# Idle 256-column products on TensorE where the schedule lets it rest, in a transformer, router and scan block

## The chip, the cores and the metric

The kernel runs on one core of a Trainium2 chip. The metric is the device time of one execution in microseconds (us), the lowest being best. Three executions of the kernel before gave 2063.22, 2063.66 and 2065.26 us, so their median is 2063.66 us. The profile is of a further execution.

## The reference, cut to what matters

Sixteen sequences of 512 tokens and 256 features pass through four stages, each with a residual addition on a freshly normalised input:

```python
x = x + attention(layernorm(x))     # 16 heads of 16, causal softmax, rms norm inside
x = x + ffn(layernorm(x))           # base + shared low rank + 6 routed low-rank experts, best 2 of 6
x = x + ssm(layernorm(x))           # conv of 4, gates, a scan over 512 steps with state 16 x 256
x = x + ffn(layernorm(x))           # the same weights again
```

All data is float32. The sequences are independent of each other; within one, every stage needs the one before it.

## The kernel before, in words

The whole program is unrolled. For each sequence the functions `attention`, `routed`, `scan` and `routed` again record *operations*: a `Plan.op` has an engine, an estimated cost, a function that issues its instructions, and the tiles that it reads and writes. Nothing is issued while they are recorded. Then `Plan.order()` plays all operations of all sequences through a small model of the core: each engine does one operation at a time, an operation is ready when those it depends on are done, places in SBUF and PSUM are counted, and of the ready ones an engine takes the one with the lowest *turn* (`STARTS` of its sequence plus a number from `TURNS`). The operations in the order of their starts in that model are the program: the loop under `tc.manual_schedule()` calls their functions one by one, and each engine's queue runs in that order. The model's times decide the order and nothing else[...].

Four setup functions run in that last loop, each ahead of the first operation of its stage. `for_attention` (ahead of the first operation of stage 2) loads and scales weights and issues a small transpose (L359) and two products `wo` by `sg` (L474) on TensorE. They are not in the model.

TensorE (PE) writes two kinds of places in PSUM: `one`, four buffers of one bank each (128x512 float32), and `sc`, a single place of four banks. The operations that matter below:

- `turned`: four transposes of a normalised sequence (`xhA`, `xhR`) by `ident` into a `one` (L505), which ScalarE (ACT) copies to `xtA`, `xtR` or `xpad` (L508).
- `four`: scores of four heads into `sc`, L566, and masks, L568. In the first use VectorE (DVE) reduces the scores to `negm` (L637). In the second, ACT takes the exponent into `pt` (L585). The next `four` needs `sc` again, so these alternate with it.
- `turn` of `negm` (L645), then `qm` on DVE (L650); `weigh`, the weighted values (L590); `back` (L601).
- In `scan`: GpSimd (POOL) multiplies at L856 and L867 on `dd`, which arrives by DMA from `drows`; ACT's exponent L861; DVE's scan L864; and `add`, eight PE instructions at L874 for two `dd`, after which the `dd` are free for the next transfers.
- `products` (L474) are all plain matrix products; a float32 product is recorded as two matmul instructions.

The PE estimate in the model is `pe(n, k) = k * 2 * (n / 1200 + 0.02)` us, a transpose group is 0.66, and `act(512)` is 0.63. The first PE operation of the plan is sequence 0's `turned`. Ahead of it the model knows: the load of `x`, 0.7 us of issue, 2.3 of transfer and 2.0 of latency; four times 0.6 us of statistics; 1.65 us of POOL; four times 0.593 us of ACT.

Of the kernel before, what the change touches and what calls it, by code (L numbers as in the profile page):

```python
# [10 lines left out]
F32 = mybir.dt.float32  # L11
# [6 lines left out]
P = 128  # L18
# [31 lines left out]
class Buf:  # L50


    def __init__(self, plan, res, make):
        self.plan, self.res, self.make = plan, res, make
        self.tile, self.users, self.taken = None, 0, False
        self.done = {}
# [11 lines left out]
class Plan:  # L68
# [6 lines left out]

    def __init__(self, places):
        self.places, self.ops, self.seq, self.stage = dict(places), [], 0, 0

# [45 lines left out]
    def order(self):  # L126

        first = {}
        for o in self.ops:
            o.turn = STARTS[o.seq] + (TURNS or [0] * len(self.ops))[o.num - first.setdefault(o.seq, o.num)]  # L130
        free, busy, table, link, port = dict(self.places), {}, None, 0.0, False
        kept = {}
        ready = {}
        for o in self.ops:
            ready.setdefault(o.eng, [])
            busy.setdefault(o.eng, False)
            if not o.left:
                bisect.insort(ready[o.eng], (o.turn, o.num, o))
        events, out = [], []
        now, tick = 0.0, 0  # L140
        while True:
            for eng, heap in ready.items():
                if busy[eng] or not heap:
                    continue
                until, what = kept.get(eng, (None, None))

                picked, turns = None, heap
                if eng == "ACT":
                    turns = sorted(heap, key=lambda i: (i[0] + CHANGE * (i[2].table not in (None, table)), i[1]))
                for item in turns:  # L150
                    if until is not None and not self.wanted(item[2], what):
                        cost = item[2].cost + 1.3 * (item[2].table not in (None, table))
                        if now + cost > until + OVER:
                            continue
                    need = {}
                    for b in item[2].bufs:
                        if not b.taken:
                            need[b.res] = need.get(b.res, 0) + 1
                    if not (item[2].port and port) and all(free[k] >= v for k, v in need.items()):
                        picked = item[2]  # L160
                        heap.remove(item)
                        break
                if picked is None:
                    continue
                o = picked
                for b in o.bufs:
                    if not b.taken:
                        b.taken = True
                        free[b.res] -= 1
                cost = o.cost  # L170
                if o.table is not None:
                    cost += 1.3 * (o.table != table)
                    table = o.table
                if until is not None and self.wanted(o, what):
                    del kept[eng]
                if isinstance(o.then, Op):
                    kept[o.then.eng] = (now + cost + o.lat, o.then)
                elif o.then is not None:
                    kept[o.then[0]] = (now + cost + o.lat, o.then[1])
                busy[eng] = True  # L180
                port = port or o.port
                out.append(o)
                end = now + cost
                done = end + o.lat
                if o.load:
                    link = max(link, end) + o.load
                    done = link + o.lat
                tick += 2
                heapq.heappush(events, (end, tick, "free", o))
                heapq.heappush(events, (done, tick + 1, "done", o))  # L190

            late = [eng for eng, (at, what) in kept.items() if at + 0.3 < now and not busy[eng]]
            for eng in late:
                del kept[eng]
            if late:
                continue
            if not events:
                if not kept:
                    break
                kept.clear()  # L200
                continue
            now = events[0][0]
            while events and events[0][0] <= now:
                _, _, kind, o = heapq.heappop(events)
                if kind == "free":
                    busy[o.eng] = False
                    if o.port:
                        port = False
                    continue
                for b in o.bufs:  # L210
                    b.users -= 1
                    if not b.users:
                        free[b.res] += 1
                for x in o.after:
                    x.left -= 1
                    if not x.left:
                        bisect.insort(ready[x.eng], (x.turn, x.num, x))
        assert len(out) == len(self.ops), "operations wait for each other's places"
        self.span = now
        return out  # L220


@with_exitstack
def tile_block(ctx: ExitStack, tc: tile.TileContext, a: dict, out: bass.AP):
# [4 lines left out]
    nc = tc.nc  # L229
# [16 lines left out]
    ps = ctx.enter_context(tc.tile_pool(name="ps", bufs=1, space=PSUM))  # L246
# [5 lines left out]
    def tile_of(name, shape, dtype=F32):  # L252
        return const.tile(shape, dtype, name=name)
# [7 lines left out]
    ident, identb = tile_of("ident", [P, P]), tile_of("identb", [P, P], BF)  # L261
# [166 lines left out]
    banks = {"one": (4, [P, 512]), "sc": (1, [P, G, 512])}  # L428
# [3 lines left out]
    plan = Plan(places)  # L432
# [463 lines left out]
    with tc.manual_schedule():  # L896
        done = 0
        for o in plan.order():

            while done < o.stage:  # L900
                setups[done]()
                done += 1
            o.fn()


# [44 lines left out]
```

## Time and profile before

| | |
|---|---|
| median of the runs | 2063.66 us |
| profiled execution, its own time | 2066.51 us |
| its span, first to last instruction | 2064.7 us |
| mean granted TensorE clock | 0.954 |
| PE busy | 1801.9 us, 87% |
| DVE / POOL / ACT busy | 1513.4 / 1371.1 / 1194.0 us |

The profiled execution is 2.85 us above the median of the three, and 1.8 us of its own time lie outside its span. "PEclk" in a table of stretches is the TensorE clock that was granted, as a share of full speed, meaned over the stretch. In a list of instructions, a row has its start, its time, engine, line, what it wrote and read, and in brackets how long the engine had been idle before it and which instruction ended that. Rows of the same line that follow closely are merged, and "x8" is their number; ends of matmuls are modelled.

### The profile page before, as it was taken

The numbers are of one execution on the slowest core, as the hardware profiler recorded it, in microseconds if no ns is written. First come the engines' busy times: TensorE is split into PE (matmuls) and PEld (weight loads), VectorE is DVE, ScalarE is ACT, GpSimd is POOL, SyncE is SP. The second block draws the span as 40 slices with busy tenths as digits, with TensorE's granted clock in tenths as the row PEclk, the third lists the DMA queues.
The fourth block names the chain that finished last, engine by engine and source line by source line (L and its number), as shares of the span: only waits on it lengthen the run. The fifth ranks groups of instructions, "written<-read, shape, count | busy, mean of one in ns | idle before, by whom it ended". The sixth has DMA issues, their size and how long they took to land. (4 is left out here: it accounts for less than half of the span.)

```text
span 2064.7 us, 34733 instructions
## 1 busy us (share of the span) xinstructions
PE 1801.9 (87%) x13253; PEld 953.8 (46%) x13253; DVE 1513.4 (73%) x2479; ACT 1194.0 (58%) x1685; POOL 1371.1 (66%) x814
## 2 busy tenths in 40 slices
PE   4788789999999999999999999999999999996455
PEld 2244344555455454545455454545554454544123
DVE  4335677878788787878788787878788787876563
ACT  2236556565666757565666667575666766564431
POOL 3001784949587685859597785859596785848693
PEclk8789899999999999999999999999999999998766
DMA  3000956848494866847494867849493957747791
GB/s 93 1 1 22 216 122 155 197 127 210 109 233 109 216 164 167 205 137 191 110 231 100 225 153 175 204 120 212 110 231 95 228 143 186 183 125 183 186 222 31
DMA packets 113064, 316.35 MB, mean 153 GB/s; under 512 B 17809, under 2 KB 36610, under 8 KB 112898
## 3 DMA queue, kind: packets, MB, share of 16 engines
q1 hardware_dynamic: 112194, 313.99, 62.5%
q8 instruction: 105, 1.72, 0.4%
q14 instruction: 61, 0.50, 0.1%
q10 hardware_dynamic: 704, 0.14, 0.0%
HBM read 287.87 MB, written 26.21 MB: 152 GB/s over the span
## 5 line engine op out<-in xcount | busy, mean ns | idle before, releaser
L864 DVE TENSOR_TENSOR_SCAN dd<-one,dd 128x512 f32<-128x512 f32 x512 | 607.9, 1212 | 185.2 <-ACT one L861 88.3
L856 POOL TENSOR_TENSOR dd<-dd,bc 128x1024 f32<-128x1024 f32 x256 | 603.6, 2361 | 194.0 <-DMA dd<-drows 156.8
L867 POOL TENSOR_TENSOR dd<-dd,bc 128x1024 f32<-128x1024 f32 x256 | 601.9, 2358 | 86.2 <-DVE dd L864 80.4
L637 DVE TENSOR_REDUCE negm<-sc 128x4 f32<-128x512 f32 (+3 forms) x256 | 380.4, 1486 | 154.0 <-PE sc L568 153.7
L861 ACT ACTIVATE one<-dd,am 128x512 f32<-128x512 f32 x512 | 344.3, 689 | 249.4 <-DVE dd L864 108.9
L585 ACT ACTIVATE pt<-sc 128x2048 f32<-128x2048 f32 (+3 forms) x256 | 316.3, 1235 | 189.0 <-PE sc L568 187.8
L487 POOL TENSOR_SCALAR rs<-mv 128x4 f32<-128x4 f32 x64 | 12.3, 193 | 364.2 <-DVE mv L482 361.4
L566 PE MATMUL sc<-qm,kT 32*128 32x512 f32 (+3 forms) x2048 | 214.1, 488 | 37.8 <-ACT pt L585 28.4
L566 PE MATMUL sc<-kT,qT 32*128 32x128 f32 (+3 forms) x2048 | 217.0, 494 | 30.5 <-DVE negm L637 25.9
L568 PEld LDWEIGHTS <-identb 128*128 128x128 bf16 x2048 | 117.4, 98 | 232.4 <-issue 217.2
L874 PE MATMUL one<-dd,ysel 128*32 128x512 f32 x1024 | 172.7, 633 | 55.5 <-POOL dd L867 46.4
L590 PE MATMUL one<-pt,vv 128*32 128x512 f32 (+3 forms) x2048 | 191.6, 449 | 8.1 <-DVE dd L864 7.9
L566 PEld LDWEIGHTS sc<-qm,kT 32*128 32x128 f32 x2048 | 80.9, 185 | 181.5 <-ACT pt L585 120.4
L474 PE MATMUL one<-base,xtR 128*128 128x256 f32 x512 | 139.5, 395 | 18.6 <-DVE dd L864 18.0
L566 PEld LDWEIGHTS sc<-kT,qT 32*128 32x128 f32 x2048 | 82.0, 187 | 156.8 <-DVE negm L637 63.3
L494 ACT ACTIVATE xhR<-x,nm,rs 128x256 f32<-128x256 f32 x192 | 99.4, 588 | 53.2 <-POOL nm L490 53.1
L528 DVE TENSOR_TENSOR x<-one,x 128x512 f32<-128x512 f32 x128 | 86.4, 675 | 34.7 <-PE one L474 34.5
L474 PEld LDWEIGHTS one<-base,xtR 128*128 128x128 f32 x512 | 94.5, 194 | 36.8 <-DVE dd L864 21.5
L481 DVE BATCH_NORM_STATS2 st<-x 128x6 f32<-128x256 f32 x256 | 103.7, 405 | 4.8 <-DMA x<-in_x_dram 4.1
L568 PE MATMUL sc<-mask_q,identb 128*128 128x128 bf16 x1024 | 103.7, 225 | 0.0
L568 PE MATMUL sc<-mask_k,identb 128*128 128x128 bf16 x1024 | 102.8, 224 | 0.0
L505 PE MATMUL one<-ident,xhR 128*128 128x128 f32 x384 | 61.9, 290 | 35.2 <-ACT xhR L494 27.7
(132 smaller groups left out, 2449.4 us busy)
## 6 DMA issues: line engine op xcount, KB each, us to landing
dd<-drows SPq DMA_DIRECT2D x512, 512.0 KB
x<-in_x_dram SPq DMA_DIRECT2D x16, 512.0 KB
drows<-dt SPq DMA_DIRECT2D x32, 256.0 KB
drows<-sg SPq DMA_DIRECT2D x32, 256.0 KB
bc<-brows SPq DMA_DIRECT2D x16, 512.0 KB
out_dram<-x SPq DMA_DIRECT2D x16, 512.0 KB
brows<-few SPq DMA_DIRECT2D x16, 64.0 KB
wo<-in_Wo_dram SPq DMA_DIRECT2D x2, 256.0 KB
```

Source lines behind the costliest of these rows:

```text
L474: nc.tensor.matmul(o[:, lo:hi], lhsT=lhsT, rhs=rhs, start=n == 0, stop=n == len(todo) - 1)
L481: nc.vector.bn_stats(st()[:, t, :], x()[:, t, :])
L566: nc.tensor.matmul(sc()[:, g, 0:n], lhsT=lhsT(g), rhs=rhs(g), start=True, stop=False)
L568: nc.tensor.matmul(sc()[:, g, at : at + P], lhsT=identb, rhs=mask, start=False, stop=True)
L585: o.then = op("ACT", act(G * n), lambda pt=pt, sc=sc, n=n: nc.scalar.activation(pt(), sc()[:, :, 0:n], AF.Exp), r=[sc], w=[pt], table="exp")
L590: nc.tensor.matmul(av()[rows(g), kt * P : T], lhsT=vals()[:, kt, G * j + g, :], rhs=pt()[:, g, :], start=kt == 0, stop=kt == NT - 1,)
L637: o.then = op("DVE", dve(G * n), lambda t=t, n=n, sc=sc, nm=nm, s=s: nc.vector.tensor_reduce(nm()[:, t, :, 1 - s, 0:1], sc()[:, :, 0:n], A ...
L856: op("POOL", pool(1024), lambda dd=dd: nc.gpsimd.tensor_tensor(dd()[:, :, 1, :], dd()[:, :, 1, :], both(0), ALU.mult), port=True, r=[(bc, ...
L861: op("ACT", act(512) + 0.07, lambda i=i, k=k, dd=dd, dec=dec: nc.scalar.activation(dec(), dd()[:, i, 0, :], AF.Exp, scale=am[:, k + 4 * i ...
L864: op("DVE", 1.22, lambda i=i, dd=dd, dec=dec: nc.vector.tensor_tensor_scan(dd()[:, i, 1, :], dec(), dd()[:, i, 1, :], 0.0, ALU.mult, ALU.a ...
L867: op("POOL", pool(1024), lambda dd=dd: nc.gpsimd.tensor_tensor(dd()[:, :, 1, :], dd()[:, :, 1, :], both(1), ALU.mult), port=True, r=[(bc, ...
L874: nc.tensor.matmul(sums()[rows(g), :], lhsT=ysel[:, m, :], rhs=four[g]()[:, g % 2, 1, :], start=m == 0, stop=m == 3)
```

## The change

`order()` also notes when PE begins and ends each operation in the model (`runs`), and how many `one` places are free at each time (`room`). After the plan is made, `resting` walks through PE's rests in the model. At a point of a rest it looks back 3.4 us. If the model's PE was busy for less than 72% of that, idle products put there included, if the rest has 0.55 us left, and if a `one` place is free throughout those 0.55 us, it books one idle product of 0.45 us; otherwise it moves on by 0.1 us. The count is kept with the PE operation that ends the rest. The issuing loop puts that many products ahead of it, each into a fresh `one` tile: `ident` as weights, `ident` twice (256 columns) as the moving operand. Nothing reads the result. The order of the other operations is unchanged, and no idle product is issued before the first setup. Since the loop over setups stands ahead of the new lines, products booked ahead of the first PE operation stand behind `for_attention`'s own PE work in PE's queue.

```diff
+    SPAN, BUSY, IDLE, EDGE = 3.4, 0.72, 0.45, 0.1
...
+        runs, room = [], [(0.0, free["one"])]
...
+                if eng == "PE":
+                    runs.append((now, end, o))
...
         self.span = now
+        self.rests = self.resting(runs, room)
         return out
+
+    def resting(self, runs, room):
+
+        rests, last, at, k = {}, [], 0.0, 0
+        for begin, end, o in runs:
+            while at + self.IDLE + self.EDGE <= begin:
+                while k + 1 < len(room) and room[k + 1][0] <= at:
+                    k += 1
+                i, free = k + 1, room[k][1]
+                while i < len(room) and room[i][0] < at + self.IDLE + self.EDGE:
+                    free = min(free, room[i][1])
+                    i += 1
+                last = [x for x in last if x[1] > at - self.SPAN]
+                worked = sum(b - max(a, at - self.SPAN) for a, b in last)
+                if free > 0 and worked < self.BUSY * self.SPAN:
+                    rests[o.num] = rests.get(o.num, 0) + 1
+                    last.append((at, at + self.IDLE))
+                    at += self.IDLE
+                else:
+                    at += self.EDGE
+            last.append((begin, end))
+            at = max(at, end)
+        return rests
...
             while done < o.stage:
                 setups[done]()
                 done += 1
+            for _ in range(plan.rests.get(o.num, 0) if done else 0):
+                one = ps.tile([P, 512], F32, tag="one", name="one", bufs=banks["one"][0])
+                nc.tensor.matmul(one[:, 0 : 2 * P], lhsT=ident, rhs=ident.unsqueeze(1).to_broadcast([P, 2, P]), start=True, stop=True)
             o.fn()
```

More of the change, by code (lines that the diff above doesn't have):

```diff
@@ L169, in order @@
                         free[b.res] -= 1
+                        if b.res == "one":
+                            room.append((now, free["one"]))
                 cost = o.cost
@@ L213, in order @@
                         free[b.res] += 1
+                        if b.res == "one":
+                            room.append((now, free["one"]))
                 for x in o.after:
```

## The prediction

> **What bounds the kernel now.** I read the page's slices first, then the same by stretches for PE alone, to see where TensorE has work and at what clock.
>
> ```profile
> core 0: us, PE busy (x), PEclk, DMA share, GB/s
> 0.00:22.33 22.33, 3.64 (x13) 1.00 0.70 195
> 22.33:118.00 95.67, 69.59 (x438) 0.71 0.03 5
> 118.00:300.00 182.00, 152.39 (x1189) 0.94 0.41 97
> 300.00:1850.00 1550.00, 1456.72 (x11085) 1.00 0.69 168
> 1850.00:2028.00 178.00, 98.72 (x472) 0.74 0.80 189
> 2028.00:2064.70 36.70, 20.86 (x76) 0.73 0.04 15
> ```
>
> From 300 to 1850 us PE is busy 94% at full clock: PE bounds, and nothing about the clock can be won. The clock is lost at both ends. Next the stretches of 3.41 us around the first loss:
>
> ```profile
> 39.40:42.81 3.41, 1.47 (x12) 1.00 0.02 5
> 42.81:46.22 3.41, 1.35 (x12) 0.50 0.00 0
> ...
> 59.88:63.29 3.41, 2.96 (x13) 0.50 0.00 0
> 63.29:66.70 3.41, 3.41 (x8) 0.50 0.00 0
> 66.70:70.12 3.42, 2.86 (x30) 1.00 0.00 0
> ```
>
> The clock is either 1.00 or 0.50 and changes on a grid of 3.41 us. A stretch busy 43% (1.47 us) is followed by half speed; at half speed one busy 87% (2.96) is still followed by half speed, a full one by full speed. I laid this grid over the trace: at full clock every stretch under 50% was followed by a fall, none over 55%; at half clock nothing under 86% was followed by a rise. So keeping warm needs little more than half, warming up needs nearly all. By the grid the half clock holds 42.8 to 66.7, 76.9 to 80.4, 94.0 to 117.9; 20 us in three pieces from 213 to 292; from 1882 on, most of the time.
>
> What it costs is seen in the list of DVE, whose reductions follow `four`:
>
> ```profile
> 42.29 2.29 DVE L637 TENSOR_REDUCE negm<-sc 128x4 f32<-128x2048 f32 x1 [1.56 <-PE sc L568]
> 46.02 0.69 DVE L637 TENSOR_REDUCE negm<-sc 128x4 f32<-128x512 f32 x1 [1.44 <-PE sc L568]
> 48.58 1.23 DVE L637 TENSOR_REDUCE negm<-sc 128x4 f32<-128x1024 f32 x1 [1.87 <-PE sc L568]
> 52.10 1.76 DVE L637 TENSOR_REDUCE negm<-sc 128x4 f32<-128x1536 f32 x1 [2.29 <-PE sc L568]
> 56.58 2.29 DVE L637 TENSOR_REDUCE negm<-sc 128x4 f32<-128x2048 f32 x1 [2.72 <-PE sc L568]
> ```
>
> DVE and PE alternate: each waits for the other (one place `sc`), so PE's time is all on the path. The same shape makes DVE wait 1.56 us warm and 2.72 cold. At the end, the chain of waits runs from 1957 to 2028 through POOL and the `dd` transfers, and after 2028 mostly through PE.
>
> [...]
>
> **The change part by part.**
>
> *One product's cost.* It is two matmul instructions of 128x256 float32. Two such (`up` by `hT`) start at 293.92 and the next at 294.35: 0.43 us warm. Cold, four (`base`) start at 2052.83 and the next at 2054.54: 0.86 for two. The booked 0.45 fits the warm one. Nothing reads the result, so no other engine gets work. SP, POOL and DMA queues are passed by nothing; no transfer is added.
>
> *How many.* I applied the rule to the rests of PE in the trace, which stand in for the model's: some 175 products, about 19 before the first PE operation, 30 more up to 300 us, none from 300 to 1800, 120 after. Since the first stage runs cold in the trace and warm in the model, it gets more: I take 190. The dense middle then costs nothing, because PE never rested 28% of 3.4 us there; the cover is the rest itself. If the model's rests lie elsewhere, 15 products of 0.43 on the path are 6.5 us: bounds 0 to +6.5, taken 0.
>
> *The first batch, a loss.* In the model PE rests until the first `turned`, at 0.7+2.3+2.0+2.4+0.12+1.65+0.12+2.37+0.05 = 11.7 us. By the rule this gives six products, a pause of 1 us, six, pause, six, pause, one: 19. On the chip they stand behind the setup's PE work, which waits for weights:
>
> ```profile
> 18.93 2.08 PE L474 MATMUL one<-wo,sg 128*128 128x256 f32 x4 [0.64 <-DMA cw<-in_conv_w_dram]
> 20.80 1.80 PE L505 MATMUL one<-ident,xhA 128*128 128x128 f32 x8
> ...
> 32.37 0.50 PE L566 MATMUL sc<-kT,qT 32*128 32x128 f32 x8
> ```
>
> The transposes were ready (the last `xhA` ended at 10.85) and started as PE became free, so here 19 products are wholly on the path: two cold, 17 warm after the grid point at 22.3, 1.7+7.3 = 9.0 us. Part comes back, as PE is warm from then on. Transposes from 29.8, the first group 0.6; ACT copies 0.59, does four `xhA` (2.07) and copies 0.58: 33.7; three 512-column products of 4x0.43 (one stretch cold before): 38.9 instead of 32.4. **Loss 6.5 us**, bounds 4 and 9.
>
> *The first two heads' groups, a gain.* Cold waits of DVE before the four reductions: 1.44+1.87+2.29+2.72 = 8.3. Warm: 1.56 for the longest, 1.14 for 1024 columns (the reduction at 87.92); I estimate 1.35 and 0.9 for the others in proportion: 5.0. Gain 3.4. Waiting for L645 0.65 to 0.5. The next `four` starts at 60.33 and ACT's `pt` at 62.99, 2.66 instead of about 1.56: 1.1. Then `wq` cold delays the next `four` to 66.41, 3.4 after `pt` began, where `pt` itself needs 1.9: 1.5. Together 6.1; the stretch from 94 to 118 has the same rows: 12.2. At 76.9 to 80.4 a `four` 0.55 and a `weigh` 0.85. **Gain 13.6 us**, bounds 9 and 14. Products don't eat it: a rest of 2.4 us (DVE's 2.29) takes three, 1.3 us, and leaves 1.1, so windows stay above 60%. Had the clock fallen, three are 2.6 us and fill the rest, and the next window warms. What is late next is DVE itself, which this count already includes.
>
> *118 to 300.* 20 us cold with the same `four` rows at 214 to 223 (two of 512, 2.3 us) and shorter ones; PE isn't dense. I take **2 us gain**, bounds 0 and 4. The lead then carries through the dense middle, as order and waits there are the same.
>
> *The tail before 2028.* POOL is busy 85% of 1850:2028 and the DMA share is 0.80, so PE is off the path; only ACT's waits for cold PE in sequence 15's preparation touch it. **1 us**, bounds 0 and 3; a product batch delaying `add` could release `dd` later, about +1.
>
> *The tail after 2028.* Cold against warm rows: `add` 0.95, `wo` by `gate` 1.05, transposes 0.85, `low` 1.3, `hsc` 0.5, the last `base`/`up` 1.95: 6.6 us if all were warm. The rests before them are
>
> ```profile
> 2040.97 2.03 PE L505 MATMUL one<-ident,xhR 128*128 128x128 f32 x8 [5.57 <-ACT xhR L494]
> ...
> 2051.87 1.17 PE L754 MATMUL one<-ident,hsc 128*113 128x128 f32 x4 [5.06 <-DVE hsc L745]
> ```
>
> About eight products each, but they all run at the start of the rest, since they wait for nothing, and some 2 us stay idle at its end. A grid window falls if 1.7 us of it are idle: for 2.1 us of rest that is 2.1/3.41, six in ten. So I take 45% of 6.6: **3 us**, bounds 0 and 6.5.
>
> Sum: +6.5 −13.6 −2 −1 −3 = **−13.1 us**. The profiled execution's span goes from 2064.7 to 2051.6; its own time, 2066.51, stands 2.85 above the median, and 2063.66−13.1 gives 2050.5.
>
> **Rivals.** (a) *The first batch without the return*, slower. Products of `ident` may not count as activity, or the rests fall otherwise: then the 6.5 to 9 us ahead of the first transpose stay, nothing comes back, 2070 to 2073. For it: the batch is certain, and the path is bare there. Against: cold runs of plain products ended the half clock at 66.7 and 117.9. It decides once less than half of the 13.6 is regained. (b) *Held warm everywhere*, the tail too, and a first batch that costs 4: +4−13.6−4−3−6.5 = −23, 2040.5. Against it is the idle end of each rest. (c) *Gain at the start only, and the dense middle pays*: +6.5−13.6+6.5 = −0.6, 2063: products ahead of `four`, which needs no `one`, wait for a `one` that the model thought free. For it: the model isn't the chip; against: no rest of the trace's middle meets the rule. (d) The diff doing nothing is excluded, as the first rest alone books products.
>
> **How the numbers follow.** The forecast 0.60 (2043 to 2058); (b) 0.15; (c) 0.11; (a) and products in front of other work 0.14. 0.2%, 4.1 us, is about what a measurement of this kernel can tell from no change. Faster by more: forecast, (b) and a little of (c), 0.77; within 0.10; slower 0.13. The range takes in (b), its bounds, and (c): 2037 to 2066.
>
> **What would show it.** Right: PE clock near 1.00 from 22 to 118; the first L505 near 29.8 and the first L566 near 39, but L637 of the second head's group with waits of 1.56 for 2048 columns; the middle's PE rows unchanged; the tail's clock between 0.75 and 0.9, mean above 0.98. Wrong: the first L505 near 21 (batch not on the path), a half clock between 43 and 67, new products with waits for ACT or DVE between 300 and 1850, or POOL waiting longer for `dd` after 1940.

## The result and the profile after

The change made the kernel slower: 2083.17 us (median of 4) against 2063.44, a ratio of 1.0093 with a 95% interval of 1.0076 to 1.0110. The profiled execution took 2082.81 us, its span is 2081.0, and its mean TensorE clock rose from 0.954 to 0.983. Ratios are given beside the medians; where the two differ slightly, the ratio decides.

The stretches of PE in the kernel after (length, busy time and instructions, granted clock, DMA share, GB/s):

```profile
22.33:118.00 95.67, 81.16 (x599) 1.00 0.03 5
118.00:300.00 182.00, 160.21 (x1248) 0.97 0.42 102
300.00:1850.00 1550.00, 1458.45 (x11095) 1.00 0.69 169
1850.00:2028.00 178.00, 131.76 (x584) 0.87 0.72 170
2028.00:2064.70 36.70, 27.20 (x121) 0.81 0.09 22
```

The start is warm throughout, as wanted, and the dense middle has the same PE work as before, 1458 us against 1457. The clock of the tail is better as well (0.87 and 0.81, from 0.74 and 0.73), yet the tail is where the time went. The DMA share of 1850:2028 fell from 0.80 to 0.72, which alone says little: the early-only kernel below, which is faster than before, has 0.73 there, as its stages stand at other times.

To find the place I matched the 13253 matmuls of before with the same ones of after, idle products left out, and took the difference of their starts: +6.8 us at the first `four`, −7.1 at 124 us, −9.6 at 300, −10.1 at 1860, and then +25 at an `add` near 2021 of before's trace, +19 at 2035. So the change wins 10 us at the start, carries them through 1550 us without losing any, and loses nearly 30 in the last 200: 35 up to that `add`, of which the end gives some back.

The start, as PE's list shows it:

```profile
20.76 9.44 PE L941 MATMUL one<-ident 128*128 128x256 f32 x38
30.04 1.04 PE L541 MATMUL one<-ident,xhA 128*128 128x128 f32 x8
...
39.13 0.50 PE L602 MATMUL sc<-kT,qT 32*128 32x128 f32 x8
```

19 products (two instructions each) stand ahead of the first transpose and take 9.3 us of the bare path. What follows runs at a clock of 1.00 up to 118 us. These are DVE's reductions of the second head group, whose waits had been 1.44, 1.87, 2.29 and 2.72 us:

```profile
52.27 0.69 DVE L673 TENSOR_REDUCE negm<-sc 128x4 f32<-128x512 f32 x1 [0.92 <-PE sc L604]
54.10 1.23 DVE L673 TENSOR_REDUCE negm<-sc 128x4 f32<-128x1024 f32 x1 [1.14 <-PE sc L604]
56.67 1.76 DVE L673 TENSOR_REDUCE negm<-sc 128x4 f32<-128x1536 f32 x1 [1.35 <-PE sc L604]
59.99 2.29 DVE L673 TENSOR_REDUCE negm<-sc 128x4 f32<-128x2048 f32 x1 [1.56 <-PE sc L604]
```

The waits between 1860 and 2050 us in the kernel after (who waited for whom, us in total, times, longest):

```profile
ACT one L897 <- PE one L941: 48.3, 7, 10.0
PE one L941 <- DVE dd L900: 44.0, 13, 6.8
```

Neither line could stand there before, as L941 is new. Idle products wait for scans, and ACT's exponents wait for idle products. The list of all engines shows how, between 2012 and 2025 us:

```profile
2011.53 4.64 DVE L900 TENSOR_TENSOR_SCAN dd<-one,dd 128x512 f32<-128x512 f32 x4 [6.73 <-POOL dd L892]
2012.79 0.69 ACT L897 ACTIVATE one<-dd,am 128x512 f32<-128x512 f32 x1 [0.97 <-DVE dd L900]
...
2014.01 10.18 PE L941 MATMUL one<-ident 128*128 128x256 f32 x32 [3.56 <-DVE dd L900]
...
2023.37 2.73 ACT L897 ACTIVATE one<-dd,am 128x512 f32<-128x512 f32 x4 [9.89 <-PE one L941]
2024.12 1.06 PE L910 MATMUL one<-dd,ysel 128*32 128x512 f32 x8
2024.14 4.57 DVE L900 TENSOR_TENSOR_SCAN dd<-one,dd 128x512 f32<-128x512 f32 x4 [7.98 <-ACT one L897]
```

A place of `one` holds the exponent (L897) until the scan (L900) has read it. Sixteen products stand ahead of the `add`. The batch can begin when PE has a rest, but its products need places that scans still hold, so PE idles 3.56 us first, runs the batch until 2024.2, and only then the `add`. The next exponents come after the batch in the program and need the places that it passes through: ACT sits idle 9.89 us, then DVE 7.98 us. Half of the chain of waits from 2006 to 2050 is L941, and 36.8% are `dd` transfers. The chain shows how the two hang together, as the late `add` is followed by the issue and the transfer of the next `dd`:

```profile
2015.26 8.93 PE one L941 x30
2024.19 1.05 PE one L910 x8
...
2025.28 0.51 SPq L885
...
2025.83 6.69 DMA dd<-drows
```

POOL's waits for `dd` transfers between 1940 and 2050 us rose from 3.4 us before to 14.2, one of the signs of being wrong that the prediction had named.

### The profile page after: what moved, and what is told of

Its sections match the earlier page's. It is cut to its first block, busy times and chain, and to the rows that moved or that the text cites. A ratio compares the mean times of both kernels' runs of the same rounds, so it can differ in the third digit from the quotient of the medians.

```text
span 2081.0 us, 35605 instructions
## 1 busy us (share of the span) xinstructions
PE 1872.6 (90%) x13689; PEld 1024.0 (49%) x13689; DVE 1511.7 (73%) x2479; ACT 1194.3 (57%) x1685; POOL 1372.0 (66%) x814
## 5 line engine op out<-in xcount | busy, mean ns | idle before, releaser
L900 DVE TENSOR_TENSOR_SCAN dd<-one,dd 128x512 f32<-128x512 f32 x512 | 607.9, 1212 | 199.5 <-ACT one L897 104.2
L897 ACT ACTIVATE one<-dd,am 128x512 f32<-128x512 f32 x512 | 343.9, 689 | 272.8 <-DVE dd L900 99.6
L602 PE MATMUL sc<-kT,qT 32*128 32x128 f32 (+3 forms) x2048 | 210.8, 481 | 19.3 <-DVE negm L673 14.5
L941 PE MATMUL one<-ident 128*128 128x256 f32 x436 | 128.0, 441 | 47.3 <-DVE dd L900 44.3
L910 PE MATMUL one<-dd,ysel 128*32 128x512 f32 x1024 | 156.2, 604 | 12.7 <-issue 7.7
L941 PEld LDWEIGHTS one<-ident 128*128 128x128 f32 x436 | 90.6, 220 | 81.5 <-issue 36.5
```

The source lines that it names most:

```text
L602: nc.tensor.matmul(sc()[:, g, 0:n], lhsT=lhsT(g), rhs=rhs(g), start=True, stop=False)
L897: op("ACT", act(512) + 0.07, lambda i=i, k=k, dd=dd, dec=dec: nc.scalar.activation(dec(), dd()[:, i, 0, :], AF.Exp, scale=am[:, k + 4 * i ...
L900: op("DVE", 1.22, lambda i=i, dd=dd, dec=dec: nc.vector.tensor_tensor_scan(dd()[:, i, 1, :], dec(), dd()[:, i, 1, :], 0.0, ALU.mult, ALU.a ...
L910: nc.tensor.matmul(sums()[rows(g), :], lhsT=ysel[:, m, :], rhs=four[g]()[:, g % 2, 1, :], start=m == 0, stop=m == 3)
L941: nc.tensor.matmul(one[:, 0 : 2 * P], lhsT=ident, rhs=ident.unsqueeze(1).to_broadcast([P, 2, P]), start=True, stop=True)
```

## The experiments

Each was timed beside the kernel before. In text, "+24.7 us" is the ratio minus one, times the median of before beside it.

**Only the early, only the late products.** The rule gets a bound on the model's time: 63 products are booked early, 155 late.

```diff
-                if free > 0 and worked < self.BUSY * self.SPAN:
+                if free > 0 and worked < self.BUSY * self.SPAN and at < 1000.0:    # late: at >= 1000.0
```

> Only the 63 idle products that the model books before its 1000 us; the 155 later ones are left out. Theory A (the loss lies in the tail: a product waits for a place of `one` that a scan still holds, and a batch of up to 20 then runs ahead of an `add` that was ready): the lead of the start stays, some 10 us, so 2053 us (2051 to 2056), and the tail looks as before. Rival B (the products slow the kernel wherever they stand, or the lead is worth nothing once the transfers bound the end): 2060 to 2075.

Measured: 2056.08 us against 2061.16, ratio 0.9974 (0.9965 to 0.9984), −5.4 us: a gain, at the upper edge of what theory A forecast.

> Only the 155 idle products after the model's 1000 us. Theory A: the loss of the tail alone, without the lead of the start: 2063.4 plus 28 to 30, so 2092 us (2087 to 2096). Rival C (the tail is only late because the start shifted how the last sequences meet): the tail products alone cost little or gain, 2060 to 2070.

Measured: 2087.37 us, ratio 1.0120 (1.0104 to 1.0137), +24.7 us. So the two halves have opposite signs, and their sum, +19.3, is the change's own +19.2. B and C fall: the early products gain by themselves, and the loss needs no shifted start. The gain is smaller than the profiles said, since the profiled execution of before was a slow one of its kind (last section).

**Narrow products.** The columns go from 256 to 16.

```diff
-                nc.tensor.matmul(one[:, 0 : 2 * P], lhsT=ident, rhs=ident.unsqueeze(1).to_broadcast([P, 2, P]), start=True, stop=True)
+                nc.tensor.matmul(one[:, 0:16], lhsT=ident, rhs=ident[:, 0:16], start=True, stop=True)
```

> All 218 idle products at the same points, each with 16 columns instead of 256, so each takes a place of `one` but hardly any time of TensorE. Theory A1 (the time of the batch that runs late is the loss): no warming, so no lead; the first batch costs about 2 us; the tail loses little: 2066 us (2062 to 2071). Theory A2 (taking the places is the loss: products wait for scans, and ACT's exponents wait for places behind products): the tail still loses most of its 28 us, 2080 to 2092.

Measured: 2095.72 us, ratio 1.0162 (1.0145 to 1.0179), +33.4 us, outside both. The experiment didn't do what it should; PE's list says why:

```profile
20.69 8.13 PE L941 MATMUL one<-ident 128*128 128x16 f32 x38
...
33.32 2.93 PE L510 MATMUL one<-xtA,wq 128*128 128x512 f32 x3
```

38 instructions with a sixteenth of the columns still take 8.13 us, 0.21 each. The weight loads beside such products stay: at 2014.51 of this run, 24 of them are busy 5.20 us beside 24 products that take 5.30. So it neither removed the time nor warmed: three `wq` instructions behind them take 2.93 us, where four took 1.98 in the kernel after (33.79). The clock of 22 to 118 us reads 0.82, against 1.00 with 256 columns, and even that is too high, since this profile has no record of the clock ahead of 36.7 us and counts that time as full. The run shows roughly what the change would cost without its warming, and can't tell A1 from A2.

**Places without time.** The late products as one small bfloat16 matmul each.

```diff
-                nc.tensor.matmul(one[:, 0 : 2 * P], lhsT=ident, rhs=ident.unsqueeze(1).to_broadcast([P, 2, P]), start=True, stop=True)
+                nc.tensor.matmul(one[:, 0:16], lhsT=identb, rhs=identb[:, 0:16], start=True, stop=True)
```

> The 155 late products only, each as one bfloat16 matmul of 16 columns by the bfloat16 identity: every place of `one` is taken as before, with hardly any time of TensorE. (The narrow float32 products had kept their time: 38 instructions took 8.13 us ahead of the first transpose.) Theory A1 (the time of a batch that starts late is the loss): 2060 to 2067 us. Theory A2 (taking the places is the loss): over 2075, up to 2090.

Measured: 2064.72 us against 2062.37, ratio 1.0007 (0.9999 to 1.0015). No loss that can be told from none. The waits from 1860 to 2050 us of this kernel, of the late products at full width, and of the kernel before:

```profile
PE one L941 <- DVE dd L900: 43.1, 13, 7.1
ACT one L897 <- PE one L941: 6.7, 3, 3.0
...
ACT one L897 <- PE one L941: 45.7, 6, 9.9
PE one L941 <- DVE dd L900: 44.8, 13, 6.3
...
PE one L874 <- POOL dd L867: 43.4, 13, 7.2
```

PE waits for the scans as long as it does with products at full width, and the time is the same as before: there, the `add` had itself waited as long for what POOL makes of those scans. What is gone are ACT's waits, 6.7 us instead of 45.7. Here the waiting for a place is harmless by itself; a long batch that runs after the wait is not.

**One place for a batch.** The late products at full width, but all products of a batch write the same tile.

```diff
+            n = plan.rests.get(o.num, 0) if done else 0
+            if n:
+                one = ps.tile([P, 512], F32, tag="one", name="one", bufs=banks["one"][0])
-            for _ in range(plan.rests.get(o.num, 0) if done else 0):
-                one = ps.tile([P, 512], F32, tag="one", name="one", bufs=banks["one"][0])
+            for _ in range(n):
```

> The 155 late products of full width, but a batch writes one single place of `one` again and again: one place is taken for a batch in the stead of up to 20. Theory A1: each batch still waits for one place and then runs 5 to 9 us ahead of the `add`; ACT's exponents find three places: a part of the 25 us is left, 2066 to 2080. Theory A2: the loss is gone, 2053 to 2063.

Measured: 2067.69 us, ratio 1.0032 (1.0018 to 1.0046), +6.6 us. The 155 products still take PE 85.5 us, and 18 of the 24.7 us are gone. So PE's time alone isn't the whole loss either: most of the net loss arises where a long batch goes through all four places. But 6.6 us is what is left after the end has gained from its warmth. By the profiles (table in the next section) this kernel loses 12.9 us ahead of the last `add`, where the late products in four places lose 27.5. What is left is seen in PE's list and ACT's wait of this kernel:

```profile
2009.69 10.20 PE L943 MATMUL one<-ident 128*128 128x256 f32 x32 [6.11 <-DVE dd L900]
...
2019.82 1.07 PE L910 MATMUL one<-dd,ysel 128*32 128x512 f32 x8
...
2028.34 1.30 ACT L897 ACTIVATE one<-dd,am 128x512 f32<-128x512 f32 x2 [10.90 <-DMA dd<-drows]
```

The `add` behind the batch frees its two `dd` late, and the next transfers with them: ACT waits 10.90 us for one, where before its longest such wait was 4.4.

**Without the batches ahead of `add`.** Late products in batches, 74 of 155.

```diff
-                op("PE", pe(512, 1, 0.18), add, r=[four[0], four[2]], w=[sums])
+                adds.add(op("PE", pe(512, 1, 0.18), add, r=[four[0], four[2]], w=[sums]).num)
...
-            for _ in range(plan.rests.get(o.num, 0) if done else 0):
+            for _ in range(plan.rests.get(o.num, 0) if done and o.num not in adds else 0):
```

> The late products in batches as in the change, without the 81 that stand ahead of an `add`; 74 are left, ahead of transposes and projections. Theory A1 with the chain through `dd` (a late `add` keeps `dd` from the next transfer): the loss is gone, what remains warms the end: 2052 to 2063 us. If the batches ahead of transposes are as harmful, since they too hold up ACT's exponents and the adds behind them: 2066 to 2080.

Measured: 2069.56 us against 2062.01, ratio 1.0031 (1.0023 to 1.0038), +6.4 us. The first expectation misses: batches ahead of transposes and projections do harm too. In this kernel's profile they wait 18.6 us for scans, and ACT's exponents wait once for one of them, 9.2 us.

**At most three in a batch.** Of the late products, 49 are left.

```diff
-            for _ in range(plan.rests.get(o.num, 0) if done else 0):
+            for _ in range(min(3, plan.rests.get(o.num, 0)) if done else 0):
```

> At most three late products ahead of one PE operation (49 instead of 155), placed as in the change. Theory A1: a batch that starts late now holds PE for 1.3 us (2.6 cold) instead of up to 9: 2055 to 2065. If one late product is enough to break the overlap: over 2070.

Measured: 2064.36 us, ratio 1.0013 (1.0001 to 1.0024), +2.7 us. Waits of products for scans are as long as ever (44.4 us, 11 times); with about 1.3 us of batch behind each, nearly all of the loss is gone. There are fewer products too, so this run alone doesn't tell length from number.

**Each product at its time.** `order` returns the model's start of each operation, `resting` a list of times, and the issuing loop puts a product where its time falls among the operations of all engines.

```diff
-                    rests[o.num] = rests.get(o.num, 0) + 1
+                    rests.append(at)
...
-        for o in plan.order():
+        for begun, o in plan.order():
+            while idle < len(plan.rests) and plan.rests[idle] < begun:
+                idle += 1
+                if not done:
+                    continue
+                one = ps.tile([P, 512], F32, tag="one", name="one", bufs=banks["one"][0])
+                nc.tensor.matmul(one[:, 0 : 2 * P], lhsT=ident, rhs=ident.unsqueeze(1).to_broadcast([P, 2, P]), start=True, stop=True)
```

PE's order is the change's, apart from the setup's own work and nine products of the first rest, which fall ahead of the first setup and are left out; what differs is which place a product gets and whom that makes wait.

> The same 218 rests, but each product is issued in the program where the model's time of it stands among all engines' operations, not in one batch ahead of the PE operation that ends the rest. Products before the first setup are left out, the others of the first rest stand ahead of the setup's PE work. Theory A: places are then taken in the order that the model assumed, a product waits for no scan that is issued after the rest began, the first batch is off the path: start lead 10 plus 6, tail between no change and -5: 2045 us (2040 to 2053). Rival D (PE's time for the products in the tail is the loss, wherever they are issued): 2065 to 2080.

Measured: 2039.03 us, ratio 0.9890 (0.9875 to 0.9906), −22.7 us: better than both kernels, and better than expected. Its waits from 1860 to 2050 us:

```profile
ACT one L898 <- PE one L941: 39.4, 19, 6.8
...
PE one L941 <- DVE dd L901: 10.0, 10, 1.8
```

Products wait for scans 1.8 us at most, and ACT's waits are split over 19. Their total is hardly below the 45.7 us of the late products in batches, so the total of ACT's waits for products isn't the measure of the loss; ACT's waits for `dd` transfers fall to 2.3 us from 29.7 before. In the first rest:

```profile
1.34 7.55 PE L941 MATMUL one<-ident 128*128 128x256 f32 x20 [1.34 <-POOL ident masks.py:199]
```

Ten products now run while the weights are still on their way, and the batch ahead of the first transpose is gone.

**The tail in time; the start without its first batch.** The in-time version with `at >= 1000.0`, and the change with `12.0 < at < 1000.0`, which leaves 44 early products, in batches.

> Of the version that issues each product where the model's time of it stands, the products after the model's 1000 us only. The tail alone, then: from the profile of all of them, which gained 8 us between 1873 us and the end, 2053 us (2050 to 2058). If those 8 us hang on the shifted start, 2058 to 2066.

Measured: 2053.20 us against 2062.37, ratio 0.9961 (0.9945 to 0.9977), −8.0 us. The same 155 products that cost 24.7 us in batches gain 8.0 in time. Rival D falls: PE's time for them isn't the loss, and neither is their number.

> The early products as in the change, without the 19 ahead of the first PE operation; none late. By the prediction's step the first batch costs 6.5 us (4 to 9), so 2056 less 6.5, 2049.5 us (2047 to 2052). If the batch pays for itself by warming the first projections, 2054 to 2058.

Measured: 2047.85 us, ratio 0.9931 (0.9918 to 0.9944), −14.2 us. With the first batch the gain was 5.4, without it 14.2, so the batch costs some 9 us. In PE's list the first `four` starts at 30.81, against 39.13 after the change: with only the three products in the short rest behind the first transposes, `wq` and `wk` take 1.98 and 3.60 us, as after the change; in the kernel before they took 3.37 and 3.95. −14.2 and −8.0 make −22.2, close to the in-time version's own −22.7.

**The threshold of the in-time version.** `BUSY` at 0.9 and 0.55.

> The in-time version with a threshold of 0.9 instead of 0.72, 286 products instead of 218. The clock held already at 0.992, so little can be won: 2036 to 2042 us. If products in the tail are still in the way of real work, worse with their number: 2043 to 2055.

> The in-time version with a threshold of 0.55, 154 products. In the trace of before, windows above 55% kept the clock. If the model's rests are the chip's, 2037 to 2043 us; if they differ, windows fall under a half and part of the clock is lost: 2043 to 2052.

Measured: 2040.38 us, ratio 0.9894 (0.9880 to 0.9909), and 2040.56, ratio 0.9896 (0.9880 to 0.9912). Neither can be told from 0.72. Mean clocks of 0.993, 0.992 and 0.984 go with 286, 218 and 154 booked products. With the products issued in time, their number hardly matters here: the medians at the three thresholds lie within 1.6 us.

## Why the prediction was wrong

**Right in its steps, too large: the start.** The first batch stood on the path, the transposes began at 30.0 (forecast 29.8), the first `four` at 39.1 (38.9), the reductions' waits fell to 0.92, 1.14, 1.35 and 1.56 (0.9, 1.14, 1.35, 1.56). The lead at 300 us was 9.6 where the first three terms, +6.5 −13.6 −2, give 9.1, against the same profiled execution. That near agreement holds for this one execution, which had a long cold start. Over several runs the start with the batch is worth 5.4 us, and without it 14.2. Rival (a) had it that products of `ident` might not bring the clock up. With those of 256 columns the clock was 1.00 from 22 to 118 us, against 0.71 before.

**Right: the middle.** No product was issued between 300 and 1800 us, and the lead stayed. Rival (c) had put waits for a free place there, ahead of `four`. Such waits came, but in the tail: 44.0 us of them for scans between 1860 and 2050.

The next table gives two stretches of the profiles, in us: from the matmul that stands at 1860.07 in before's trace to the last four instructions of the last `add` (2028.68 there), and from these to the end of the span.

| kernel | up to the last `add` | after it |
|---|---|---|
| before | 168.6 | 36.0 |
| the change | 199.7 | 31.4 |
| late products only | 196.1 | 30.2 |
| late products, one place for a batch | 181.5 | 30.2 |
| late products, each at its time | 163.4 | 31.6 |

**Right: the end after the last `add`.** It went from 36.0 to 31.4 us, a gain of 4.6; forecast was 3, with bounds 0 and 6.5. Single profiles of kernels without late products have 34.2 and 37.3 there, so this is no closer a test than some 2 us.

**Wrong: the tail before 2028.** The step read "PE is off the path", "1 us", bounds 0 and 3, with "about +1" for a late `dd`. Measured against it is a loss of 31.1 us in the change's profile, and +24.7 us over the runs for the late products as a whole, after the end's gain. I took PE to be off the path because POOL and the transfers were busy. But PE's `add` frees the `dd` that those transfers fill, and ACT's exponents need places of `one`. The sentence that failed stands in the next step and underlies this one too: the products "all run at the start of the rest, since they wait for nothing". They have no input to wait for, but each takes one of four places, in program order. The loop issues a batch just ahead of the operation that ends the rest, so behind all exponents issued during that rest. The products then get places that these exponents still fill. The model's `room` asked whether a place was free at the product's own time in the rest; it didn't ask who takes it in the program's order. The number of products, 218 instead of 190, is not the cause, since the same 155 late ones gain when each is issued at its time.

The prediction had the pieces: "a product batch delaying `add` could release `dd` later", and a rival with waits in front of real work. The waits before the change (ACT's L861 on DVE's L864, 108.9 us) showed that `one` places are what ACT and DVE hand to each other in the scan. I priced a product as 0.43 us of PE, and left its place out of the sum: no term of the tail stood for a product that waits, or for what waits behind it, but the "about +1". What the clock itself is worth before 2028 is a few us at most, not far from the forecast: with the products out of the way the stretch takes 163.4 us, against 168.6 before and 166.0 and 166.3 in the two kernels with early products alone.

What stays open: how the 24.7 us divide between ACT's exponents and the late `add`. The one-place version leaves 6.6 us in the end, 12.9 ahead of the last `add`, but it changes both at once.

## What to carry to other kernels

Filler work is free only if everything that it takes is free, its buffer as much as its engine; look at who gets that buffer next in program order. A batch ahead of the operation that ends a rest runs late by as long as it waits (3.56 us in the list from 2012 to 2025), so issue fillers at their own times in the program. In this tail the same fillers gained 8.0 us when they were issued so, and cost 24.7 in batches.

## What had not been expected of the hardware

- Float32 products of 16 columns take PE three quarters of the time of those of 256, not a sixteenth. Over the whole program the 436 narrow instructions keep PE busy for 96.8 us, the 436 wide ones of the kernel after for 128.0, at mean clocks of 0.948 and 0.983. The first 38 take 8.13 and 9.44 us; behind the narrow ones a `wq` instruction takes 0.98 us, behind the wide ones 0.50.
- The narrow products didn't warm: from 22 to 118 us PE was busy 79.5 of 95.67 us with them, at a clock of 0.82 at most, and 81.2 us with wide ones, at 1.00. PE's busy share of the stretch, 83% and 85%, doesn't tell the two apart.
- The start differs from run to run of the same instructions. Three kernels that have before's program up to its tail (late bfloat16 products; one place; without the batches ahead of `add`) start the last transpose of `xhA` at 1708.4, 1703.7 and 1704.0 us, against 1708.7 before. The difference is there early: their first transposes of `avs` start at 80.1, 77.3 and 77.8, against 80.1 before. The clock from 22 to 118 us reads 0.71 in before's profile, 0.75 and 0.77 in the first two. Comparing one profile with one profile overstated the start's gain by about 4 us.
